# Two-layer convolution block on one core: DRAM buffers cut along their readers, and the inlaid convolution's loads moved from SyncE's queue to ScalarE's

## The chip, the core and the metric

The kernel runs on one core of a Trainium2 chip. The metric is device time in microseconds (us) of one execution; lower is better. Five engines work side by side, each through its own instructions in order: TensorE (PE, with weight loads PEld), VectorE (DVE), ScalarE (ACT), GpSimd (POOL) and SyncE (SP), which here only issues transfers. ACT and POOL issue transfers too. A transfer that must wait for something holds up the engine that issues it, and all that stands behind it there.

## The reference

An input x of 8 x 96 x 96 x 192 passes two blocks, each with a residual. All is float32.

```python
def ema_scan(x, axis):            # s = 0.6 * s + 0.4 * x_t, along one axis
    ...
def block0(x):                    # W_in: 192 -> 384, conv_w: depthwise 3x3, W_out: 384 -> 192
    proj = jnp.einsum('bhwd,dc->bhwc', gn(x), W_in) + b_in
    local = depthwise3x3(proj, conv_w)
    mixed = 0.25 * (lr + rl + tb + bt) + local     # four scans of local: both ways along w and h
    normed = layernorm(mixed, eps=1e-5) * ln_g + ln_b
    return x + jnp.einsum('bhwc,cd->bhwd', normed, W_out) + b_out
def block1(x):                    # 7x7 depthwise on 192 channels, then 192 -> 768 -> 192
    y = depthwise7x7(gn(x), dw_kernel) + dw_bias
    y = layernorm(y, eps=1e-6) * ln_gamma + ln_beta
    y = gelu(jnp.einsum('bhwc,cd->bhwd', y, w0) + b0)
    return x + (jnp.einsum('bhwd,dc->bhwc', y, w1) + b1) * gamma
# gn: 32 groups of 6 channels, over height, width and group, per image, eps=1e-5
```

## The kernel before

The work runs in five stages, with DRAM buffers between them because each stage wants another axis on the partitions.

**First pass (A).** For each image b (8 of them) and each quarter k of the row blocks, x is normalized, turned and multiplied by W_in. `store_a` (L417 and L435) writes the result `po` to the DRAM buffer `P_d`. One `P_d` holds all: two groups g of four images, 384 channels (three parts m of 128), rows and halo rows. POOL issues the writes. For the very last `po` the parts m go out on POOL, POOL and SP, and the halo row on SP.

**3x3 convolution and scans (B).** 96 steps k of four channels. `load_b(k)` asks SP for a weight band (L608) and the input `pin` (L613): per image group g the 32 rows and two halo rows. Convolutions (L626) go to ACT (L635), then to two scans on DVE (L659, L668), each 128 x 768 elements. Three steps are asked for ahead.

**Layer norm and W_out (C).** The result goes to `X1_d`.

**7x7 convolution, first half (D).** The convolution works on 32 blocks n, 16 for each half hf of the images; a block is 12 channels (two groups). A block takes three raw tiles (`load_raw`, t = 0, 1, 2: two transfers each, L839), a weight band (`load_band`, L849), 24 scalings to `xin` (L871 on ACT, L873 on DVE), a copy of the band to the other half of the partitions (`spread`, L877, DVE), six convolution steps (`conv_d`, L1196, evacuated by ACT to `yo`, L1206) and the store of `yo` to `Y_d[hf]` (`store_d`, L1222 to L1227, six transfers on SP). The first N1 = 19 blocks run alone.

**Two-layer network (E), with the other 13 blocks inlaid.** 36 tiles n of y, two rounds u each. `load_y` asks SP for 40 transfers (L1255, L1261) into `ya` and `yb`, each double-buffered. The norm's steps run mostly on DVE (its first is `sums`, L1338) one tile ahead; `turn_in` (L1386, DVE) turns y; `first_layer` (L1401, L1411) makes hp, ACT applies gelu (L1420), `second_layer` (L1431) follows, and DVE adds the residual (L1442). A round has five places where `slot()` is called. While blocks are left, `slot()` takes the next entry of the list `slots`: nine entries per block, three for the scalings and six for the convolution steps. It then takes up to seven steps of the list `loads`, which holds the y transfers that are due.

The order on each engine is the order of these calls (`manual_schedule`); there is no other planner. A tile that reuses memory waits for the last reader of what lay there. In the inlaid stretch SP's one queue therefore carries, in this order of calls, raw tiles, y pieces, bands, residual tiles r (L1276) and stores. The late blocks have two raw buffers, one band, one xin and one yo:

```python
slots[-3].append(lambda n=n: load_raw(n, NT - 1))
if more:
    for t in range(NT - 1):
        slots[t - 2].append(lambda n=n, t=t: load_raw(n + 1, t))
```

Of the kernel before, what the change touches and what calls it, by code (L numbers as in the profile page):

```python
# [8 lines left out]
F32 = mybir.dt.float32  # L9
# [92 lines left out]
def conv_blocks_kernel(  # L102
# [41 lines left out]
    GS = D // GROUPS  # L144

    const = ctx.enter_context(tc.tile_pool(name="const", bufs=1))
    dram = ctx.enter_context(tc.tile_pool(name="dram", bufs=1, space=DRAM))
# [4 lines left out]
    NJ = S // RB  # L152
    P_d = dram.tile([NG, C, RB + 2, GB, NJ, S], F32, name="P_d")
    CS = 2 * C // 3
# [13 lines left out]
    ]  # L168
    Y_d = [dram.tile([ROWS, GROUPS, NH, NV, GS * WQ], F32, name=f"Y_{hf}") for hf in range(2)]

# [33 lines left out]
    ab_pool = ExitStack()  # L204
    mp = ab_pool.enter_context(tc.tile_pool(name="ab_const", bufs=1))
    mix = mp.tile([128, NJ, 128], F32, name="mix")
# [31 lines left out]
    with ExitStack() as ph:  # L238
        cp = ph.enter_context(tc.tile_pool(name="a_const", bufs=1))
        xp = ph.enter_context(tc.tile_pool(name="a_x", bufs=6))  # L240
        sp = ph.enter_context(tc.tile_pool(name="a_small", bufs=2))
        tp = ph.enter_context(tc.tile_pool(name="a_t", bufs=2))
        op = ph.enter_context(tc.tile_pool(name="a_out", bufs=2))
        zp = ph.enter_context(tc.tile_pool(name="zprep", bufs=1))
        ps_t = ph.enter_context(tc.tile_pool(name="a_ps_t", bufs=2, space=PSUM))
        ps_m = ph.enter_context(tc.tile_pool(name="a_ps_m", bufs=2 * NC, space=PSUM))

        avg = cp.tile([S, 128], F32, name="avg")
        nc.vector.memset(avg, 1.0 / S)
        win = cp.tile([128, 3, C], F32, name="win")  # L250
        for p, k, c in spans:
            nc.scalar.dma_start(win[p, k], W_in[c])
        bin_ = cp.tile([128, NC], F32, name="bin_")
        with nc.allow_non_contiguous_dma(reason="one bias per partition"):
# [157 lines left out]
        def store_a(po, b, k):  # L412
            at, g = b % GB, b // GB
            final = b == B - 1 and k == NK - 1

            def whole(m, eng):
                eng.dma_start(  # L417
                    P_d[
                        g, m * 128 : (m + 1) * 128, k * WA : (k + 1) * WA, at
                    ].rearrange("p r j h -> p r (j h)"),  # L420
                    po[:, m].rearrange("p r j h -> p r (j h)"),
                )

            whole(0, nc.gpsimd)
            if not final:
                for m in range(1, NC):
                    whole(m, nc.gpsimd)

            for edge, r, row, js in (
                (NK - 1, WA - 1, RB, (0, NJ - 1)),  # L430
                (0, 0, RB + 1, (1, NJ)),
            ):
                if k == edge:
                    to = slice(1 - js[0], NJ - js[0])
                    (nc.sync if final else nc.gpsimd).dma_start(  # L435
                        P_d[g, :, row, at, to].rearrange("(m p) j h -> p m (j h)", p=128),
                        po[:, :, r, js[0] : js[1]].rearrange("p m j h -> p m (j h)"),
                    )
            if final:
                for m in range(1, NC):  # L440
                    whole(m, (nc.sync, nc.gpsimd)[m % 2])

        def zero_edge(i):

            g, m, e = i // (2 * NC), i // 2 % NC, i % 2
            nc.gpsimd.dma_start(
                P_d[g, m * 128 : (m + 1) * 128, RB + e, :, e * (NJ - 1)], zero
            )
# [49 lines left out]
        with tc.manual_schedule():  # L498
# [13 lines left out]
            for b in range(B):  # L512
                more = b + 1 < B
                for t in range(n_t):
# [40 lines left out]
                    if j == NJ - 1:  # L555
                        store_a(po, b, k)
                if more:
# [12 lines left out]
    NI = len(place)  # L570
    by_tile = dict(reuse_waits="tile")
    gn_pool = ExitStack()
# [15 lines left out]
    with ExitStack() as ph:  # L588
# [12 lines left out]

        def load_b(k):
            c = slice(k * CC, (k + 1) * CC)
            band = bp_.tile([128, CC, 3, RB], F32, tag="band", name=f"band0_{k}")
            pin = bp_.tile([128, CC, GB, NJ, S], F32, tag="pin", name=f"pin_{k}")
            for g in range(NG):
                p = g * 64
                nc.sync.dma_start(  # L608
                    band[p : p + RB + 4].rearrange("p c t o -> p (c t o)"),
                    ZB_d[:, c].rearrange("r c t o -> r (c t o)"),  # L610
                )
                for lo, hi in ((0, RB), (RB, RB + 1), (RB + 1, RB + 2)):
                    nc.sync.dma_start(  # L613
                        pin[p + lo : p + hi].rearrange("p c b j h -> p c (b j h)"),
                        P_d[g, c, lo:hi].rearrange("c r b j h -> r c (b j h)"),
                    )
            return band, pin

# [73 lines left out]
        with tc.manual_schedule():  # L692
            loads = [load_b(k) for k in range(3)]
            locs, lasts, zs, mos, todo = {}, {}, {}, {}, []
# [119 lines left out]
    N1 = NI + 3  # L814
    d_pools = [early, None]
    raws, bands, xins, yos = {}, {}, {}, {}

    def load_raw(n, t):

        hf, i = todo[n]  # L820
        if n >= N1 or ((n == 0 or n % 2) and t < NT - 1):
            pool, bufs = early, NT - 1
        elif n == 0 or n % 2:
            pool, bufs = gp, 1
        else:
            pool, bufs = d_pools[1], NT
        raw = pool.tile([128, NH, NV, GC, WQ], F32, tag="raw", name="raw", bufs=bufs)
        raws[n, t] = raw
        row = NGC * NV * GC * WQ
        run = NV * GC * WQ  # L830
        x1 = X1_d[hf]
        engs = (nc.sync, nc.gpsimd) if n < 2 else (nc.gpsimd,) * 2 if n < N1 else (nc.sync,) * 2
        for g, eng in enumerate(engs):
            src = bass.AP(
                tensor=x1.tensor,
                offset=x1.offset + (2 * t + g) * HG * PH * row + i * run,
                ap=[[row, 64], [ROWS * row, NH], [1, run]],
            )
            eng.dma_start(  # L839
                raw[g * 64 : (g + 1) * 64].rearrange("q b a c v -> q b (a c v)"), src  # L840
            )

    def load_band(n):

# [3 lines left out]
        g = i % 2  # L848
        nc.sync.dma_start(  # L849
            band[g * 64 : (g + 1) * 64].rearrange("q c l -> q (c l)"),  # L850
# [363 lines left out]
    def store_d(n):  # L1214
# [5 lines left out]
        for k in range(2):  # L1220
            y_d = Y_d[hf][:, 2 * i + k].rearrange("r b a n -> r (b a n)")
            nc.sync.dma_start(  # L1222
# [11 lines left out]
    def load_y(n):  # L1234

        hf, p, a, j = place(n)
        y = Y_d[hf][(NJ3 - 1 - j) * PH + PH - 1 - p :: NJ3 * PH]
        main = CK // GS
# [7 lines left out]
        def piece(q, b, eng):  # L1246
# [7 lines left out]
            if b < NH:  # L1254
                eng.dma_start(  # L1255
                    dst[:, b, :cut].rearrange("i (g n) -> i g n", g=main),
                    y[:, chunk * main : (chunk + 1) * main, b, a],
                )
            else:
                g, c = divmod(chunk * (CK - main * GS), GS)  # L1260
                eng.dma_start(  # L1261
                    dst[:, :, cut:],
                    y[:, GROUPS - 2 + g, :, a, c * WQ : (c + CK - main * GS) * WQ],
                )
# [190 lines left out]
    with tc.manual_schedule():  # L1455
# [56 lines left out]
        gn_pool.close()  # L1512
        yp = ctx.enter_context(tc.tile_pool(name="e_yT", bufs=2, side="right", **by_tile))
        rp = ctx.enter_context(tc.tile_pool(name="e_r", bufs=2, side="right", **by_tile))
        tp = ctx.enter_context(tc.tile_pool(name="e_t", bufs=2, side="right", **by_tile))

        slots = []
        for n in range(N1, len(todo)):
            more = n + 1 < len(todo)
            scales = scale_steps(n)  # L1520
            per_t = len(scales) // NT
            slots += [scales[:per_t], scales[per_t : 2 * per_t], scales[2 * per_t :]]
            slots[-3].append(lambda n=n: load_raw(n, NT - 1))
            if more:
                for t in range(NT - 1):
                    slots[t - 2].append(lambda n=n, t=t: load_raw(n + 1, t))
            slots += [[lambda n=n, c=c: conv_d(n, c, ps_y)] for c in range(GS)]
            slots[-1].append(lambda n=n: store_d(n))
            if more:
                slots[-1].append(lambda n=n: load_band(n + 1))  # L1530

        loads = []

        def slot():

            if slots and u >= 2:
                for step in slots.pop(0):
                    step()
            for step in loads[:7]:
                step()  # L1540
            del loads[:7]

# [7 lines left out]
        for u in range(n_u + 1):  # L1550
# [27 lines left out]
            second_layer(u - 1, 2, pool)  # L1578
            turn_in(u + 1, 1)
            if t == 0 and n + 2 < n_y and u < n_u:  # L1580
                assert n + 2 < n_y // 2 or not slots
                assert not loads
                loads += load_y(n + 2)
            chain.pop(0)()
            slot()
            if early_half:
# [52 lines left out]
```

## Time and profile before

| | us |
|---|---|
| median of 3 runs (lowest to highest) | 5541.16 (5528.82 to 5553.41) |
| profiled execution: time | 5532.09 |
| profiled execution: span of its trace | 5530.3 |
| PE busy in the span | 5295.1 (96%) |
| DVE, ACT, POOL busy | 3600.3, 2587.0, 2317.4 |

The trace covers one execution. A busy PE row means that matmuls were under way, not that PE ran at full clock: a table by stretches of time also gives the clock that PE was granted (PEclk, 1.00 is full) and the share of the time in which the transfer engines were busy. "A <- B" in a list of waits means that A stood idle until B ended. A row "SPq" is SP issuing a transfer. Places in the span are given in us from its start: A ends near 753, B near 1790, C near 2628, the first 19 blocks of D near 2945, the inlaid blocks near 4030.

### The profile page before, as it was taken

What the parts mean: (1) busy time and instruction counts of PE and PEld (TensorE: products, weight loads), DVE (VectorE), ACT (ScalarE), POOL (GpSimd) and SP (SyncE); (2) the same over time, 40 slices, a digit from 0 to 9 for tenths busy, and PEclk for the clock granted to TensorE, in tenths of its full rate; (3) what the DMA queues carried; (4) which work ended last, traced back from release to release, by engine and by line L of the source; (5) the groups of instructions that cost most, each with busy time, mean ns of one, the idle gap of its engine ahead of it and who ended that gap; (6) DMA issues with size and microseconds to landing.
All of it is one profiled execution on the core that took longest, in us unless ns stands there. A gap on an engine that the chain in (4) does not pass through costs nothing. (4 is left out here: it accounts for less than half of the span.)

```text
span 5530.3 us, 108052 instructions
## 1 busy us (share of the span) xinstructions
PE 5295.1 (96%) x42206; PEld 3366.3 (61%) x42206; DVE 3600.3 (65%) x6722; ACT 2587.0 (47%) x5778; POOL 2317.4 (42%) x2021
## 2 busy tenths in 40 slices
PE   6999989999999999999788999999999999999999
PEld 4666643333333899899445555666566667767767
DVE  6656449999999455555556555555467777667764
ACT  2444447777777566565435444444433332332332
POOL 1111128888888455555322222222233333333332
PEclk9999989999999999999899999999999999999999
DMA  7999879999997899899996555555433233333331
GB/s 224 286 289 268 237 195 244 246 241 247 243 245 209 256 291 290 266 286 300 294 281 164 119 121 127 125 134 131 111 91 82 80 80 78 83 94 83 80 79 40
DMA packets 793774, 1015.27 MB, mean 184 GB/s; under 512 B 330623, under 2 KB 669696, under 8 KB 791216
## 3 DMA queue, kind: packets, MB, share of 16 engines
q1 hardware_dynamic: 700104, 673.23, 47.8%
q0 software_dynamic: 82976, 331.44, 18.4%
q8 instruction: 333, 5.46, 0.4%
q10 hardware_dynamic: 10184, 3.70, 0.3%
q14 instruction: 177, 1.45, 0.1%
HBM read 603.70 MB, written 419.95 MB: 185 GB/s over the span
## 5 line engine op out<-in xcount | busy, mean ns | idle before, releaser
L1431 PEld LDWEIGHTS hp<-w1g,g 128*128 128x128 f32 x6912 | 1118.6, 190 | 141.4 <-issue 74.0
L1431 PE MATMUL hp<-w1g,g 128*128 128x192 f32 x6912 | 1175.6, 329 | 0.0
L1420 ACT ACTIVATE g<-hp,b0g 128x512 f32<-128x512 f32 x864 | 518.3, 690 | 1149.9 <-PE hp L1411 1149.8
L1450 POOL DMA_DIRECT2D out_dram<-xo x288 | 210.5, 731 | 1647.9 <-DVE xo L1442 1554.0
L1401 PE MATMUL hp<-yT,w0w 128*128 128x512 f32 x1728 | 781.1, 598 | 10.8 <-DVE yT L1386 10.8
L1442 DVE TENSOR_TENSOR xo<-hp,r 128x384 f32<-128x384 f32 x288 | 227.5, 790 | 816.4 <-PE hp L1431 812.1
L1032 PE MATMUL po<-wc,mt 128*128 128x193 f32 x3456 | 688.0, 335 | 9.1 <-DVE x1c L1049 9.1
L626 PE MATMUL pl<-pin,band 34*32 34x380 f32 (+1 forms) x13824 | 628.7, 490 | 20.4 <-DMA pin<-P_d 20.4
L700 POOL TENSOR_TENSOR mo<-mo,z 128x768 f32<-128x768 f32 x286 | 597.2, 2088 | 4.4 <-ACT mo L651 0.4
L1032 PEld LDWEIGHTS po<-wc,mt 128*128 128x128 f32 x3456 | 557.3, 192 | 40.5 <-ACT mean L1034 30.2
L1196 PE MATMUL hp<-xin,band 63*64 63x372 f32 (+1 forms) x4608 | 433.4, 510 | 126.7 <-ACT yo L1206 39.6
L1401 PEld LDWEIGHTS hp<-yT,w0w 128*128 128x128 f32 x1728 | 322.5, 191 | 373.5 <-issue 337.8
L659 DVE TENSOR_TENSOR_SCAN z<-decay,loc 128x768 f32<-128x768 f32 x288 | 505.8, 1756 | 46.0 <-ACT loc L635 16.5
L668 DVE TENSOR_TENSOR_SCAN z<-decay,z 128x768 f32<-128x768 f32 x288 | 498.3, 1731 | 0.1
L626 PEld LDWEIGHTS pl<-pin,band 34*32 34x32 f32 x13824 | 232.5, 107 | 398.5 <-issue 395.8
L1365 POOL TENSOR_TENSOR rs<-tot,neg_half 32x32 f32<-32x32 f32 x72 | 394.6, 5481 | 105.0 <-DVE tot L1363 104.8
L647 PE MATMUL pa<-loc,mix 128*32 128x384 f32 x3456 | 431.9, 493 | 0.0
L650 PE MATMUL pa<-last,down 96*32 96x384 f32 x1152 | 426.8, 493 | 0.9 <-ACT mo L651 0.9
L1411 PE MATMUL hp<-yT,w0w 64*128 64x512 f32 x1728 | 419.6, 611 | 0.0
L1196 PEld LDWEIGHTS hp<-xin,band 63*64 63x64 f32 x4608 | 225.1, 141 | 304.5 <-issue 168.4
L1206 ACT ACTIVATE yo<-hp,dwb 128x384 f32<-128x384 f32 x384 | 196.2, 582 | 441.1 <-PE hp L1196 289.0
L635 ACT COPY loc<-pl 128x384 f32<-128x384 f32 x576 | 248.2, 483 | 313.0 <-PE pl L626 313.0
(155 smaller groups left out, 7519.1 us busy)
## 6 DMA issues: line engine op xcount, KB each, us to landing
pin<-P_d SPq DMA_DIRECT2D x192, 576.0 KB
P_d<-po POOLq DMA_DIRECT2D x95, 1152.0 KB, 9.7
mt<-M SPq DMA_DIRECT2D x192, 384.0 KB
xq<-in_x_dram SPq DMA_DIRECT2D x96, 576.0 KB
xr<-in_x_dram SPq DMA_DIRECT2D x192, 288.0 KB
X<-x1c SPq DMA_DIRECT2D x144, 384.0 KB
out_dram<-xo POOLq DMA_DIRECT2D x288, 192.0 KB, 2.6
r<-X SPq DMA_DIRECT2D x35, 1536.0 KB
```

Source lines behind the costliest of these rows:

```text
L626: nc.tensor.matmul(pls[g][at * RB : (at + 1) * RB, :, lo:hi], band[rows, c, kh, :], pin[rows, c, :, NJ - 1 - j, lo + kh - 1 : hi + kh - 1] ...
L647: nc.tensor.matmul(pa[at], mix[:, i, at], loc[:, q], start=True, stop=True)
L650: nc.tensor.matmul(pa[at], down[:, to], last[:, q], start=True, stop=True)
L659: nc.vector.tensor_tensor_scan(zf, decay_f, loc.rearrange("p q n -> p (q n)"), 0.0, ALU.mult, ALU.add)
L668: nc.vector.tensor_tensor_scan(zr, decay_f, zr, 0.0, ALU.mult, ALU.add)
L700: eng.tensor_tensor(m, m, z, ALU.add)
L1032: nc.tensor.matmul(po, lhs[m], wc[:, m], start=(m == 0), stop=(m == NC - 1))
L1196: nc.tensor.matmul(pys[g][k * 64 : (k + 1) * 64, :, lo:hi], band[rows, k * GS + c, d * ZS : d * ZS + 64], xin[rows, :, :, k * GS + c, lo + ...
L1401: nc.tensor.matmul(hps[m, q], w0w[:, 0, m * 128 : (m + 1) * 128], yT[:, 2 * q], start=True, stop=False,)
L1411: nc.tensor.matmul(hps[m, q], w0w[p, 1, m * 128 : (m + 1) * 128], yT[p, 1], start=False, stop=True,)
L1420: nc.scalar.activation(g[:, m, q], hps[m, q], AF.Gelu, bias=b0g[:, m : m + 1], scale=1.0)
L1431: nc.tensor.matmul(po[:, q], g[:, m, q, k * 128 : (k + 1) * 128], w1g[:, m], start=(m == 0), stop=(m == NE - 1),)
```

## The change

1. `P_d` becomes six buffers, one for each group g and part m. The last `po`'s part m = 0 goes out in two halves of 64 partitions, on POOL and on ACT, its halo row on ACT; parts 1 and 2 and their halo rows go out on POOL. Halo rows are stored for each part apart.
2. The memory pools of stage A get `reuse_waits="tile"`, `pin` gets two tags, and stage B's start asks first for group 0 of k = 0 and 1, then for group 1 of k = 0, and so on; within a step the inputs now stand ahead of the band.
3. `Y_d[hf]` becomes seven buffers: six of five groups of channels, as one y piece reads them, and one of two.
4. In the inlaid stretch the raw tiles and bands are asked for by ACT. There are three raw buffers instead of two (the third lies in the pool of yT), and all three tiles of block n + 1 are asked for during block n's scalings. Block 19's third tile is asked for by POOL at the end of D, as its first two now are.
5. `store_d(n)` moves from the end of block n's last slot to the start of the next block's first slot.
6. `slot()` takes up to 14 steps of `loads`, and `load_y` is added after the fourth slot of a round instead of before it.

```diff
-    P_d = dram.tile([NG, C, RB + 2, GB, NJ, S], F32, name="P_d")
+    P_d = [
+        [dram.tile([128, RB + 2, GB, NJ, S], F32, name=f"P_{g}_{m}") for m in range(NC)]
+        for g in range(NG)
+    ]
...
+    YG = 5
+    Y_d = [
+        [
+            dram.tile(
+                [ROWS, min(YG, GROUPS - g), NH, NV, GS * WQ], F32, name=f"Y_{hf}_{g}"
+            )
+            for g in range(0, GROUPS, YG)
+        ]
...
-        xp = ph.enter_context(tc.tile_pool(name="a_x", bufs=6))
+        xp = ph.enter_context(tc.tile_pool(name="a_x", bufs=6, **by_tile))
...
             if final:
-                for m in range(1, NC):
-                    whole(m, (nc.sync, nc.gpsimd)[m % 2])
+                whole(0, nc.gpsimd, slice(0, 64))
+                edges(0, nc.scalar)
+                whole(0, nc.scalar, slice(64, 128))
+                steps = [lambda m=m: whole(m, nc.gpsimd) for m in range(1, NC)]
+                return steps + [lambda m=m: edges(m, nc.gpsimd) for m in range(1, NC)]
...
-            loads = [load_b(k) for k in range(3)]
+            tile_b(2)
+            bands_b[0] = tile_band_b(0)
+            for k in range(2):
+                load_pin_b(k, 0)
+            for k in range(3):
+                for g in range(1 if k < 2 else 0, NG):
+                    load_pin_b(k, g)
+                load_band_b(k)
+            loads = [tiles_b[k] for k in range(3)]
+            for step in late_a:
+                step()
...
-        engs = (nc.sync, nc.gpsimd) if n < 2 else (nc.gpsimd,) * 2 if n < N1 else (nc.sync,) * 2
+        engs = (nc.sync, nc.gpsimd) if n < 2 else (eng or nc.gpsimd,) * 2
...
+        d_pools[2] = yp
+        load_raw(N1, NT - 1)
...
-            slots += [scales[:per_t], scales[per_t : 2 * per_t], scales[2 * per_t :]]
-            slots[-3].append(lambda n=n: load_raw(n, NT - 1))
+            slots += [after + scales[:per_t], scales[per_t : 2 * per_t], scales[2 * per_t :]]
             if more:
-                for t in range(NT - 1):
-                    slots[t - 2].append(lambda n=n, t=t: load_raw(n + 1, t))
+                for t in range(NT):
+                    slots[t - 3].append(lambda n=n, t=t: load_raw(n + 1, t, nc.scalar))
             slots += [[lambda n=n, c=c: conv_d(n, c, ps_y)] for c in range(GS)]
-            slots[-1].append(lambda n=n: store_d(n))
             if more:
-                slots[-1].append(lambda n=n: load_band(n + 1))
+                slots[-1].append(lambda n=n: load_band(n + 1, nc.scalar))
+            after = [lambda n=n: store_d(n)]
+        slots.append(after)
...
-            for step in loads[:7]:
+            for step in loads[:14]:
                 step()
-            del loads[:7]
+            del loads[:14]
...
+            chain.pop(0)()
+            slot()
             if t == 0 and n + 2 < n_y and u < n_u:
                 assert n + 2 < n_y // 2 or not slots
                 assert not loads
                 loads += load_y(n + 2)
-            chain.pop(0)()
-            slot()
```

## The prediction

> **What bounds the kernel now.** I read the stretch table first, one row per stage, to see where PE is not busy; then the lists of waits in those places; then the timeline of one gap. The columns after the length are busy us of PE, PEld, DVE, ACT, POOL, then the clock granted to PE, the transfer engines' share, GB/s.
>
> ```profile
> 753.00:771.00 18.00, 0.64 (x2) 0.18 (x2) 1.41 (x11) 0.57 (x2) 1.33 (x2) 0.57 0.96 268
> 771.00:1788.00 1017.00, 1014.50 (x18368) 351.16 (x18366) 974.13 (x573) 712.01 (x1716) 867.53 (x939) 0.99 0.92 238
> ...
> 2627.60:2945.00 317.40, 244.08 (x2630) 149.90 (x2628) 171.99 (x482) 126.19 (x255) 79.33 (x106) 0.90 0.96 278
> ...
> 2945.00:4030.00 1085.00, 1020.79 (x5622) 630.39 (x5623) 593.11 (x1136) 489.78 (x849) 296.63 (x153) 0.97 0.54 126
> ...
> 4370.00:5530.00 1160.00, 1154.62 (x5260) 809.85 (x5256) 773.25 (x1449) 355.92 (x499) 387.79 (x216) 1.00 0.30 78
> ```
>
> The last stretch is PE at full clock: nothing there can be won by moving transfers. Stage B (second row) is DVE's: 288 pairs of scans at 1.756 and 1.731 us are 1004 of its 1017 us, so B ends a fixed time after its first scan starts. D's first half is held by transfers (0.96). Two places are left: the 18 us between A and B, and the inlaid stretch, where PE idles 64 us and runs at a mean clock of 0.97 with the transfer engines half idle. Its waits, total us, times, longest:
>
> ```profile
> DVE s L1338 <- DMA yb<-Y: 106.6, 13, 17.7
> ...
> ACT xin L871 <- DMA raw<-X: 69.1, 13, 11.5
> ...
> PE hp L1196 <- DVE band L877: 30.3, 4, 10.9
> ...
> PE hp L1196 <- ACT xin L871: 18.8, 6, 6.4
> ```
>
> So PE waits for a block's first convolution (L1196), and behind that stand late y pieces (`sums`, L1338, blocks the band copy queued behind it on DVE) or late raw tiles. One such gap in the timeline:
>
> ```profile
> 3200.31 1.87 SPq L1255 DMA_DIRECT2D yb<-Y  x4
> ...
> 3202.28 1.25 SPq L839 DMA_DIRECT2D raw<-X  x2
> ...
> 3209.33 3.61 ACT L871 ACTIVATE xin<-raw,s 128x192 f32<-128x192 f32 x8 [6.67 <-DMA raw<-X]
> ...
> 3212.63 1.01 DVE L1338 TENSOR_REDUCE s<-yb 128x16 f32<-128x512 f32 x1 [12.49 <-DMA yb<-Y]
> 3213.67 1.45 DVE L877 COPY band<-band 64x2496 f32<-64x2496 f32 x1
> ...
> 3215.27 4.04 PE L1196 MATMUL hp<-xin,band 63*64 63x384 f32 x24 [10.16 <-DVE band L877]
> ```
>
> The reader is to see that raw tile and y pieces are interleaved in SP's one queue, both asked for late, and that the convolution after the gap takes 4.04 us; at full clock 24 such matmuls end and the next group begins after 2.06 (3567.57 to 3569.62).
>
> **What the inlaid stretch would take without gaps.** From 2991 to 4064 (1073 us) lie 26 rounds u and 13 x 6 = 78 convolution steps. A round without convolutions repeats every 32.24 us (L1431 pairs at 4087.14 and 4119.38). 26 x 32.24 + 78 x 2.06 = 999 us: 74 us are lost to gaps and to the half clock after them. A second way: PE issues 1758 matmuls in 317 us from 3495 to 3812, where it never waits over 2 us (5.55 per us), but 2546 in 504 us before (5.05) and 1289 in 252 us after (5.12); at 5.55 the outer two would take 459 and 232, that is 65 us less. Both agree on the size of what is to be had.
>
> **The change, part by part.**
>
> *A to B.* In the trace, the last `po` (ACT and DVE end at 753.6) is written, SP's loads wait and interleave with the writes, and B's first convolutions run at 774.3:
>
> ```profile
> 766.20 0.17 DVE L972 MEMSET blk<- 128x128 f32 x1 [13.18 <-DMA P_d<-po]
> ...
> 769.42 1.57 SPq L613 DMA_DIRECT2D pin<-P_d  x3
> ...
> 774.32 15.50 PE L626 MATMUL pl<-pin,band 34*32 34x384 f32 x190 [2.50 <-DMA pin<-P_d]
> ...
> 779.34 1.76 DVE L659 TENSOR_TENSOR_SCAN z<-decay,loc 128x768 f32<-128x768 f32 x1 [11.59 <-ACT loc L635]
> ```
>
> Group 0's inputs for k = 0, 1 can now land before 753 (the transfer share from 680 to 752 is 0.38 to 0.50). The critical loads, group 1 of k = 0, follow m = 0's write, which now goes on two queues and no longer has m = 2's beside it on SP's ring: written by about 758, loaded by about 764, against pieces landing until 774. But DVE has a memset ahead of the first scan, and in the changed order it (c_pre, the row after blk) waits for all last writes, m = 1 and 2 and their halo rows too, all on POOL now. By 758 about 1.5 of 3.5 MB is written; the rest shares some 330 GB/s (324 to 342 from 756 to 764) with the loads: 2.0 / 0.165 = 12 us, to about 770.5. First scan at about 770.8, against 779.34: -8.5 us, with -12 (scan follows the loads) and -5 (writes squeezed out longer) as ends. POOL issues 32 more halo stores of 0.744 us in A (24 us, beside 111 busy of 753): free, as POOL spends 533 us waiting for ACT's `po`. Were POOL full, `po`'s two buffers would hold up ACT.
>
> *Y_d.* SP's waits around the first y loads (2895 to 2992) name no store of Y for a y load: reads are already tied only to stores that they overlap. 0 (-3 to +3 for another layout of the same rows).
>
> *Raw tiles and bands to ACT, third buffer, tiles a block ahead.* 12 blocks x 6 = 72 raw transfers and 12 bands leave SP. The raw tile, now asked for a block (some 70 us) ahead, is not late; y pieces lose the raw requests standing among them. ACT gets 72 x 0.61 + 12 x 1.39 = 61 us of issuing (SP's durations), over 490 busy of 1085; in the timeline it waits 3.6 us for PE ahead of each group of four gelus, so a pair (1.2 us) fits. Against this stands a rule of the Trainium skill, "DMA: Bandwidth & Descriptors", section "Issuing engines are not separate DMA queues": all issuers end on the same 16 engines, and another issuer only saves issue time. By it the move is worth nothing here, since SP is not short of issue time, and the total is -8.5 alone, about 5533. The rows say otherwise: what is saved is not issue time but the place in the queue. SP stood in front of y loads (L1255) waiting for DVE 728 us in all, with raw requests behind, while ACT waited 69 us. I take the rows and keep the rule for the range.
>
> *What is late next.* Two things stay. In 3495 to 3812, with no late transfer, PE still gave up 3 us in 4.4 blocks, as eight scalings (3.6 us) follow four gelus (2.4 us): about 1 us a block, 13 us. And the eight transfer semaphores turn in call order over SP and ACT together: each new transfer waits for the one eight before. ACT can thus stop for a y piece that SP has not landed. A y tile takes 31 us of SP's time in the last stretch and 34 to 44 in 3495 to 3812; its last calls now stand 24 us after the buffer is free, so an ACT request just behind can wait 5 us or so. What queues behind it are gelus, then PE. Nothing in the trace shows it; below, 0 (the request meets a finished one); above, 4 us a block (a lag of 8 less the 3.6 idle). I take 1 us a block, as slots just behind the last y piece are about one in five: 12 us. So the stretch gives -74 + 13 + 12 = -49 (ends -70 and -10).
>
> *store_d a slot later, y pieces 14 at a time, load_y after the slot.* No instruction is added; DVE's and PE's order stay. The single yo has three slots (24 us) from store to next writing, and the six issues take about 5.5 us (0.33 + 0.35 + 2.05, twice): covered, and if not, ACT's yo waits (16 us now in this stretch). In the last stretch y pieces end 12 us before `sums`: covered.
>
> *Third tile of block 19 by POOL at D's end.* 2.3 MB of raw now start near 2954 beside y_1's pieces (2944 to 2977), which DVE awaits (9 us gap of PE at 2978); at 300 GB/s that is 8 us of traffic. +3 (0 to +8).
>
> **Sum.** -8.5 - 49 + 3 = -54.5, against the profiled execution's 5532.09: 5477.6. The median of the runs, 5541.16, stands 9 above that execution; on it, 5486.7. I forecast 5486 for the median.
>
> **The rivals.**
>
> 1. *All of it goes:* no request on ACT is held, as in the quietest stretch or better. -8.5 - 70 = 5463. For: transfer share 0.54. Against: ACT's bursts ahead of first convolutions remain.
> 2. *The queue was not the cause:* y pieces stay late by their own chain (yb pieces wait for each other, some 4 us per five), and only A to B and a part of raw remain: -8.5 to -20, about 5527. For: yb is the name in the longest waits. Against: from 3583 to 3697 the same chain was in time.
> 3. *ACT becomes the bound* (slower): each block's seven requests wait on SP's y pieces, gelus stand, PE drops to half clock. Its place is a block's three scaling slots; at 9 us a block (6 of gap, 3 of half clock, like the gap above less ACT's idle) 13 blocks cost 117, and 5541 - 54.5 + 117 = 5604. It decides from 54.5 / 13 = 4.2 us a block. For: ACT's queue is in order and semaphores are shared. Against: SP, freed of raws, runs ahead of the calls most of the time.
> 4. *The split does nothing:* if DVE's memset ends with the old writes' time (766) plus loads as now, A to B gives 0: 5495. Inside the first case's range.
>
> **How the numbers follow.** Likeliest case 0.63 (own range 5465 to 5508), rival 1 0.19, rival 2 0.13, rival 3 0.05. Range 5450 to 5522: below, rival 1 with A to B at -12 and a fast run; above, the weak half of rival 2 is left out. This kernel's measurement tells about 0.5% (28 us) from no change: faster by more means under 5513. Faster: 0.63 + 0.19 + 0.07 of rival 2 = 0.89; within: 0.06 of rival 2 and 0.01 of rival 3 = 0.07; slower 0.04.
>
> **What would show it.** First scan of B near 771 and its wait a memset's for the writes of P; SP's rows with no raw from 3000 on; "DVE s <- DMA yb" and "ACT xin <- DMA raw" under 20 us each; gaps of PE ahead of L1196 of 1 to 2 us, clock 0.99 in the stretch; the inlaid blocks ending near 3975 instead of 4030. Wrong: ACT rows at raw requests that wait for y transfers by more than 4 us a block, or y pieces still late with SP free.

## The result, and the profile after

The changed kernel takes 5499.89 us (median of 11 runs, 5494.79 to 5531.08), the kernel before, run beside it, 5537.92 us (11 runs, 5527.56 to 5553.70). The ratio is 0.9935, with a 95% interval of 0.9918 to 0.9953. The profiled execution took 5497.31 us (span 5495.5); that of before, 5532.09. So some 35 to 38 us went, where 54.5 were forecast.

The stretches of the changed kernel, with the same bounds and columns as those shown of before (busy us of PE, PEld, DVE, ACT, POOL; granted clock; transfer share; GB/s):

```profile
753.00:771.00 18.00, 1.81 (x12) 0.78 (x8) 2.80 (x11) 2.10 (x4) 3.57 (x5) 0.66 0.83 252
771.00:1788.00 1017.00, 1015.71 (x18368) 354.97 (x18368) 974.32 (x574) 711.82 (x1716) 868.01 (x939) 0.99 0.91 237
2627.60:2945.00 317.40, 244.43 (x2643) 148.18 (x2643) 175.86 (x491) 130.28 (x264) 80.68 (x107) 0.88 0.96 279
2945.00:4030.00 1085.00, 1042.71 (x5775) 649.16 (x5774) 580.41 (x1176) 499.39 (x858) 321.02 (x165) 0.98 0.52 127
```

Only the last row has moved much: PE issues 5775 matmuls there where it issued 5622. The list of waits for 2945 to 4030 (total us, times, longest) has no row any more of ACT's scaling waiting for a raw tile (69.1 us before):

```profile
DVE s L1388 <- DMA yb<-Y: 58.0, 9, 19.6
...
PE hp L1244 <- DVE band L925: 18.8, 1, 18.8
...
PE hp L1244 <- ACT xin L919: 3.9, 5, 1.6
```

One gap of 18.8 us still stands in it, and another of 18.4 us lies ahead of it (PE waiting for DVE's `yT`): both at E's start. From 3076 to 4030 the first of these rows is only this:

```profile
DVE s L1388 <- DMA yb<-Y: 20.5, 6, 10.2
```

To compare kernels stage by stage I use times at which DVE ends the last transpose (L1386 before, L1436 after) of a y tile. At that time its buffer is free for the y tile two later, so "y_3's buffer free" in the expectations is when y_1 has been turned (also called "y_1's free" there). All in us, read to about 0.1:

| kernel | A's last matmul to B's first scan | E's first matmul to y_0 turned | to y_1 turned | to y_13 turned | rest |
|---|---|---|---|---|---|
| before | 26.9 | 30.6 | 67.1 | 1006.3 | 1465.6 |
| after | 23.4 | 39.1 | 76.8 | 954.2 | 1466.3 |
| difference | -3.5 | +8.5 | +9.7 | -52.1 | +0.7 |

What is left of the -34.8 of the spans is +2.3 in A (PE starts at 41.5 instead of 39.85), +0.9 in B, +1.8 in C and -3.2 in D. So a gain of 52 us in the inlaid stretch was there, and 18 were given back at E's start.

**The step from A to B, after.** The timeline:

```profile
754.89 2.50 POOL L430 DMA_DIRECT2D P<-po  x3 [18.23 <-ACT po L421]
...
760.47 4.26 SPq L644 DMA_DIRECT2D pin<-P  x3
764.83 3.26 SPq L631 DMA_DIRECT2D band<-ZB_d  x2
...
772.29 8.44 PE L662 MATMUL pl<-pin,band 34*32 34x384 f32 x90 [17.48 <-issue]
774.91 0.17 DVE L1027 MEMSET c_pre<- 128x128 f32 x1 [17.09 <-DMA P<-po]
777.30 0.86 ACT L671 COPY loc<-pl 128x384 f32<-128x384 f32 x2 [21.41 <-PE pl L662]
778.19 1.76 DVE L695 TENSOR_TENSOR_SCAN z<-decay,loc 128x768 f32<-128x768 f32 x1 [3.12 <-ACT loc L671]
```

The reader is to see that the memset waits for the last writes as foretold, but is done 3 us before the scan: the scan waits for ACT's copy, and that for the convolution. What the convolution waits for this list does not name; the loads in front of it are issued from 760 on, and e2_band_first below names them.

**E's start, after.** Two events, in one timeline:

```profile
2951.16 3.73 POOL L887 DMA_DIRECT2D raw<-X  x6
...
2953.41 2.20 SPq L1305 DMA_DIRECT2D yb<-Y  x4
2972.58 0.30 SPq L1311 DMA_DIRECT2D yb<-Y  x1
...
2986.26 1.01 DVE L1388 TENSOR_REDUCE s<-yb 128x16 f32<-128x512 f32 x1 [17.73 <-DMA yb<-Y]
2994.22 2.05 PE L1451 MATMUL hp<-yT,w0w 128*128 128x512 f32 x2 [18.44 <-DVE yT L1436]
...
3030.85 15.91 SPq L1305 DMA_DIRECT2D yb<-Y  x4
...
3041.41 1.28 ACTq L887 DMA_DIRECT2D raw<-X  x2
...
3048.43 0.30 SPq L1311 DMA_DIRECT2D yb<-Y  x1
...
3059.20 1.00 DVE L1388 TENSOR_REDUCE s<-yb 128x16 f32<-128x512 f32 x1 [19.61 <-DMA yb<-Y]
3070.87 1.46 DVE L925 COPY band<-band 64x2496 f32<-64x2496 f32 x1
3072.47 3.96 PE L1244 MATMUL hp<-xin,band 63*64 63x384 f32 x24 [18.79 <-DVE band L925]
```

First event: POOL asks for block 19's raw tiles at 2951, and the next piece of y_1's yb can be asked for only 19.2 us after the first four (2953.41 to 2972.58); before, with those raws on SP behind the y pieces, 8.7 us (2957.06 to 2965.80). Whether the raws are the cause is tested below. Second event: the row at 3030.85, an ask for four pieces of y_2, takes SP 15.9 us, nearly all of it one wait ahead of the fourth. What it waits for is in SP's own list of waits (2991 to 3076):

```profile
SPq L1305 <- DMA raw<-X: 14.2, 1, 14.2
```

That piece reads and writes nothing of raw. What ties it to raw is the semaphore that tells of a transfer's landing. In the trace the transfers of SP and of ACT use the same eight in turn (numbers 100 and 102 to 108), those of POOL eight others (111 to 118). The piece has to wait for number 108, and the transfer that had it last, eight before in order of calls, is ACT's raw request. ACT issues that only at 3041.41, between two bursts of scaling.

### The profile page after: what moved, and what is told of

It is laid out like the page before. It is cut to its first block, busy times and chain, and to the rows that moved or that the text cites. A ratio compares the mean times of both kernels' runs of the same rounds, so it can differ in the third digit from the quotient of the medians.

```text
span 5495.5 us, 108054 instructions
## 1 busy us (share of the span) xinstructions
PE 5277.4 (96%) x42206; PEld 3357.6 (61%) x42206; DVE 3449.8 (63%) x6722; ACT 2586.1 (47%) x5778; POOL 2367.0 (43%) x2060
## 5 line engine op out<-in xcount | busy, mean ns | idle before, releaser
L1244 PE MATMUL hp<-xin,band 63*64 63x372 f32 (+1 forms) x4608 | 420.7, 501 | 95.7 <-ACT yo L1254 35.2
L395 PE MATMUL pm<-xT,win 128*128 128x384 f32 x1152 | 392.4, 491 | 0.0
```

Of the source, the lines that this page charges most:

```text
L1244: nc.tensor.matmul(pys[g][k * 64 : (k + 1) * 64, :, lo:hi], band[rows, k * GS + c, d * ZS : d * ZS + 64], xin[rows, :, :, k * GS + c, lo + ...
```

## Experiments

Every run is compared with the kernel before on the same chip in the same session; "run on SP" is e1_raw_sp.

**e1_p_only.** The parts for `P_d`, `store_a` and B's first loads alone, on the kernel before:

```
+        [dram.tile([128, RB + 2, GB, NJ, S], F32, name=f"P_{g}_{m}") for m in range(NC)]
...
+                whole(0, nc.gpsimd, slice(0, 64))
+                edges(0, nc.scalar)
+                whole(0, nc.scalar, slice(64, 128))
...
+            for k in range(2):
+                load_pin_b(k, 0)
...
```

> Only the first pass's buffers and the order of stage B's first loads are taken from the change; Y's buffers and the inlaid convolution stay as before. Theory (the gain is all in the inlaid stretch, and the step from A to B gave 1 to 4 us because the band of k = 0 now stands behind two waiting pin loads): first scan of B 1 to 4 us earlier counted from A's last matmul, whole time -4 to +4 us, ratio 0.9993 to 1.0007. If the later start of C seen after the change (+3.6 us) comes from this part, C's first matmul stands 3 to 5 us later here too and the ratio is near 1.0005; if it comes from elsewhere, C moves with the scan. Rival (the forecast's term, -8.5 us, was right and the other 5 us were lost elsewhere): ratio 0.9985.

Measured: 5535.19 us, ratio 0.9998 (0.9985 to 1.0011); A's last matmul to the first scan 23.5 us; the inlaid stretch 1008.4. This part is worth 3.4 us of 5540, below what whole times resolve. C starts 12.6 us later in its profiled execution, because B took 1030.8 us instead of 1017.5; the last section shows such lengths of B without these edits too.

**e1_e_only.** The inlaid edits alone, without the split of P and Y:

```
+            pool, bufs = d_pools[2], 1
+                    slots[t - 3].append(lambda n=n, t=t: load_raw(n + 1, t, nc.scalar))
+                slots[-1].append(lambda n=n: load_band(n + 1, nc.scalar))
+            after = [lambda n=n: store_d(n)]
+            for step in loads[:14]:
...
```

> Only the inlaid convolution's edits are taken (requests on ScalarE, third raw tile, a block ahead, y pieces 14 at a time, store a slot later); the DRAM buffers and stage B's loads stay as before. Theory: the whole gain is here: -52 us in the steady stretch, +16 to +20 us at E's start, so -30 to -38 us, ratio 0.993 to 0.9945. Rival (the split of Y is what frees the y pieces): -10 to -20 us, ratio 0.9965 to 0.998.

Measured: 5504.98 us, ratio 0.9942 (0.9925 to 0.9960), with 40.6, 76.7 and 954.4 us in the three stages of E: those of the changed kernel. The split of Y does nothing that shows.

**e1_raw_sp and e1_raw_pool.** The changed kernel with the inlaid raws and bands asked for by SP, and by POOL:

```
-                    slots[t - 3].append(lambda n=n, t=t: load_raw(n + 1, t, nc.scalar))
+                    slots[t - 3].append(lambda n=n, t=t: load_raw(n + 1, t, nc.sync))      # or nc.gpsimd
-                slots[-1].append(lambda n=n: load_band(n + 1, nc.scalar))
+                slots[-1].append(lambda n=n: load_band(n + 1, nc.sync))                    # or nc.gpsimd
```

> The changed kernel, but the inlaid blocks' raw tiles and bands are asked for by SP again; third raw tile, the block's lead and the y pieces' 14 at a time stay. Theory 1 (the place in SP's queue is the cause, as forecast): raws again stand among y pieces and wait for buffers there; 'DVE s <- DMA yb' comes back to 60 to 100 us, and 30 to 45 us of the gain are given back: ratio to before 0.999 to 1.002. Theory 2 (the lead of a block and the third tile are the cause, the queue is not): the steady stretch stays within 10 us of the changed kernel's, and y_2's late piece at E's start, which waited for ScalarE's raw request, comes sooner: ratio 0.990 to 0.9945.

> The changed kernel, but the inlaid blocks' raw tiles and bands are asked for by GpSimd, whose transfers count on semaphores of their own. Theory (SP's and ScalarE's shared eight semaphores hold y_2's piece behind ScalarE's raw request at E's start): the second long gap of PE at E's start (18.8 us, at about 3054) shrinks to 10 us or less, with the half clock after it: 8 to 18 us faster than the changed kernel, ratio to before 0.990 to 0.992. Rival (y_2's pieces are late from traffic and order alone, or GpSimd's requests come late behind its own waits): gap stays above 15 us, ratio 0.993 to 0.996.

Measured: SP 5479.28 us, ratio 0.9896 (0.9879 to 0.9912); POOL 5482.28 us, ratio 0.9893 (0.9877 to 0.9909). To y_1 turned: 60.0 and 59.8 us instead of 76.8; to y_13 turned: 952.2 and 951.2 instead of 954.2. Putting everything back into SP's queue loses nothing and wins 17 us at E's start. With the other edits in place, the queue in which the raw requests stand is not what gains: there the forecast's cause is refuted (e3_queue_only asks the same of the kernel before). The second gap at E's start, 18.8 us of PE, was the price of ScalarE's requests.

**e2_blk20_sp.** One request is enough to show the place of that price:

```
-   load_raw(n + 1, t, nc.scalar)
+   load_raw(n + 1, t, nc.sync if n == N1 else nc.scalar)
```

> The changed kernel, with only the first inlaid block's requests for the next block's raw tiles moved from ScalarE to SP; all later ones stay on ScalarE. Theory (the loss on ScalarE is one event: y_2's piece waits for the ScalarE request eight transfers ahead, issued late): from y_0's buffer free to y_1's free 60 to 63 us instead of 76.8, later stretch unchanged at 952 to 956, so 14 to 17 us faster than the changed kernel: ratio to before 0.990 to 0.991. Rival (the coupling meets the next block instead): the same loss appears one or two y tiles later, ratio 0.993 to 0.994.

Measured: 5479.57 us, ratio 0.9906 (0.9889 to 0.9924); 60.3 us to y_1 turned and 953.7 to y_13. Where PE waited 18.79 us it now waits 2.38:

```profile
3064.26 3.61 PE L1244 MATMUL hp<-xin,band 63*64 63x384 f32 x24 [2.38 <-DVE band L925]
```

The loss was one event, at the first block; the raw requests of the other eleven blocks and all bands, still on ScalarE, cost nothing that shows. The coupling itself goes on: from 3076 to 4064 SP's y pieces (L1305) wait for raw transfers 49.8 us in 17 waits in the changed kernel, against 15.7 us in 11 in the run on SP, for a stretch only 2 us longer.

**e3_queue_only.** The kernel before, with the move to ScalarE alone:

```
-        engs = (nc.sync, nc.gpsimd) if n < 2 else (nc.gpsimd,) * 2 if n < N1 else (nc.sync,) * 2
+        engs = (nc.sync, nc.gpsimd) if n < 2 else (nc.gpsimd,) * 2 if n < N1 else ((nc.sync, nc.scalar)[n > N1],) * 2
...
-        nc.sync.dma_start(
+        (nc.sync, nc.scalar)[n > N1].dma_start(
```

> The kernel before, with one edit: from block 20 on, raw tiles and bands are asked for by ScalarE. Third raw tile, lead and y pieces as before. Theory (the forecast's cause, SP's queue, is not it; the third tile's short lead and the y pieces' pace are): from y_3's buffer free to y_15's free 995 to 1015 us (before 1006), ratio 0.999 to 1.004. Rival (the queue is a cause too, and lead and pace are two more ways to the same gain): 960 to 985 us, ratio 0.992 to 0.997.

Measured: 5534.28 us (22 runs), ratio 1.000 (0.999 to 1.001), 1002.5 us to y_13 turned. So the move to ScalarE gives nothing in the whole and at most 4 us in its stretch. This is a balance: in the trace SP's y pieces (L1255) wait 45.7 us for raw transfers from 3076 to 4064, against 6.5 before. The same move to POOL, whose transfers share no semaphore with SP's, was not run on the kernel before; on the changed kernel POOL and SP differ by 1 us (951.2 and 952.2).

**e2_lead_only and e3_pieces_only.** The run on SP with one half of the other inlaid edits each. Lead only keeps the third raw buffer and its tile's lead of a block; besides the lines shown, `load_y` is called ahead of the slot again:

```
-            for step in loads[:14]:
+            for step in loads[:7]:
-            after = [lambda n=n: store_d(n)]
+            slots[-1].append(lambda n=n: store_d(n))
```

> As the run with raws asked for by SP, and with the y pieces 7 at a time, their start and the store's slot also put back as before: of the edits in the inlaid stretch only the third raw buffer and the third tile's lead of a block are left. Theory (that lead alone is the cause): from y_3's buffer free to y_15's free stays within 952 to 962 us (before 1006, changed 954), whole time within 8 us of the run on SP. Rival (the y pieces' rate and place hold half of it): 970 to 990 us in that stretch, 15 to 30 us slower than the run on SP.

Pieces only keeps what this undoes, and undoes what it keeps (block 19's raw tiles are asked for by SP again, too):

```
-            pool, bufs = d_pools[2], 1
-                for t in range(NT): slots[t - 3].append(lambda n=n, t=t: load_raw(n + 1, t, nc.sync))
+            slots[-3].append(lambda n=n: load_raw(n, NT - 1))
+                for t in range(NT - 1): slots[t - 2].append(lambda n=n, t=t: load_raw(n + 1, t))
```

> As the run with raws asked for by SP, but without the third raw buffer and the third tile's lead of a block: of the inlaid edits only the y pieces 14 at a time, their start a slot later and the store a slot later are left, with all requests on SP. Theory (the two parts add: lead 22, pieces 32 of 54 us): 968 to 982 us from y_3's to y_15's buffer free, ratio 0.993 to 0.996. Rival (both are needed for the gain of either beyond 22): 990 us or more, ratio over 0.997.

Measured: lead only 5511.96 us, ratio 0.9957 (0.9941 to 0.9973), 983.9 us to y_13 turned; pieces only 5511.15 us, ratio 0.9956 (0.9943 to 0.9969), 982.5 us. Against 1006.3 before, each is worth 22 to 24 us, and both together 54 (952.2): they add, with 8 us more that only both give. In the first of the two the rival I had set against "lead alone" came true (33 us slower than the run on SP, a little more than its 15 to 30); the second ended at the edge of its theory (982.5 against 968 to 982).

The waits from 3076 to 4064 tell the two apart. Before:

```profile
DVE s L1338 <- DMA yb<-Y: 91.4, 12, 17.7
ACT xin L871 <- DMA raw<-X: 62.4, 12, 11.5
...
PE hp L1196 <- DVE band L877: 21.5, 3, 10.9
```

Move to ScalarE alone:

```profile
DVE s L1338 <- DMA yb<-Y: 103.2, 12, 17.7
PE hp L1196 <- DVE band L877: 38.8, 5, 15.4
```

Lead only:

```profile
DVE s L1388 <- DMA yb<-Y: 91.1, 11, 17.2
PE hp L1244 <- DVE band L925: 23.5, 5, 9.1
```

Pieces only:

```profile
ACT xin L917 <- DMA raw<-X: 37.4, 4, 13.4
PE hp L1242 <- ACT xin L917: 24.6, 6, 8.3
DVE s L1386 <- DMA yb<-Y: 18.6, 4, 10.3
```

The reader is to see two separate troubles. Late raw tiles go with the lead; late y pieces go with the pace; the move alone took away the raw wait, and PE then waited longer for the band copy that stands behind the y pieces. Why the pieces were late is in SP's own waits of the same stretch, before, move alone, lead only and pieces only:

```profile
SPq L1222 <- ACT yo L1206: 217.4, 13, 22.0
...
SPq L1255 <- DVE yT L1386: 96.6, 7, 22.5
```

```profile
SPq L1222 <- ACT yo L1206: 212.1, 13, 19.8
```

```profile
SPq L1271 <- ACT yo L1254: 205.0, 13, 19.2
```

```profile
SPq L895 <- PE hp L1242: 199.2, 12, 40.8
...
SPq L1269 <- ACT yo L1252: 4.9, 9, 0.6
```

In the first three SP stands some 16 us a block in front of the store of Y (`store_d`), which waits for ACT's `yo`, with y pieces behind it. Before, in one block (y_4's pieces, SP alone):

```profile
3166.01 0.91 SPq L1255 DMA_DIRECT2D yb<-Y  x2
3183.24 0.32 SPq L1222 DMA_DIRECT2D Y<-yo  x1
...
3193.88 1.44 SPq L1255 DMA_DIRECT2D yb<-Y  x2
```

From first to last issue y_4's 40 pieces take 70.3 us before, and 77.2 and 69.5 in the next two. With 14 a slot and the store a slot later they are out before SP meets that store (32.0 us in the run on SP), and in pieces only SP does its waiting at the next band. Not every tile gets through so fast (y_6's pieces still take 63.0 us in the run on SP), but DVE's wait for yb falls to 18.6 us in pieces only and 28.1 on SP.

The wait for `yo` need not go for that. In the changed kernel, where the bands are on ACT, SP still stands at the store:

```profile
SPq L1271 <- ACT yo L1254: 151.3, 11, 21.6
```

Yet y_4's pieces take 31.8 us there, and the stretch is as short as on SP (954.2 and 952.2). What counts is what stands behind the wait. Which does more, the 14 a slot, `load_y` after the slot or the later store, was not run apart.

**e2_band_first.** The run on SP, band 0 ahead of group 1's pins:

```
+            first = load_band_b(0)
             for k in range(3):
                 for g in range(1 if k < 2 else 0, NG): load_pin_b(k, g)
-                load_band_b(k)
+                if k: load_band_b(k)
```

> As the run with raws asked for by SP, but at B's start band 0 is asked for ahead of group 1's pin loads, not behind them. Theory (band 0 stood behind two loads that wait for the last writes, so B's first convolution came late): from A's last matmul to the first scan 19 to 21.5 us instead of 23.8. Rival (the pin load or DVE's memset behind the last writes ends the gap anyway): 23 to 24 us, and the memset or the pin is the row's wait.

Measured: 5481.62 us, ratio 0.9913 (0.9896 to 0.9929); 24.2 us from A's last matmul to the scan, as without it. Its timeline:

```profile
763.62 6.55 SPq L646 DMA_DIRECT2D pin<-P  x6
...
773.31 12.33 PE L664 MATMUL pl<-pin,band 34*32 34x384 f32 x152 [18.39 <-DMA pin<-P]
773.64 0.17 DVE L1032 MEMSET c_pre<- 128x128 f32 x1 [16.47 <-DMA P<-po]
...
778.33 1.76 DVE L697 TENSOR_TENSOR_SCAN z<-decay,loc 128x768 f32<-128x768 f32 x1 [4.53 <-ACT loc L673]
```

The band was not the last: the pin is, issued at 763.6 after the write of m = 0 and used 9.7 us later. So that write and that load bound this step. That the load is slow because of the other writes beside it is likely, but no run tests it.

**e2_late19 and e3_blk19_sp.** The run on SP, with block 19's third tile asked for by POOL a round later; and with all three by SP, behind y_1's pieces:

```
-        load_raw(N1, NT - 1)
+            if u == 1: load_raw(N1, NT - 1)          # late19
-                load_raw(N1, t)
+                load_raw(N1, t, nc.sync)             # blk19_sp, and so for the third
```

> As the run with raws asked for by SP, but block 19's third raw tile is asked for a round later (u = 1) instead of at D's end. Theory (its 0.77 MB beside y_1's pieces cost the first rounds of E): from E's first matmul to y_0's buffer free goes from 39.6 back to 30 to 33 us, with the half clock after it 6 to 10 us in all, ratio to before 0.988. Rival (the pieces of y_1 are late by their own chain, and the first gap only moves into a wait for the raw tile at u = 2): same time within 3 us, or slower.

> As the run with raws asked for by SP, and block 19's three raw tiles are asked for by SP too, in the same place of the program: they stand behind y_1's pieces and the last stores, as two of them did before, instead of starting beside y_1's pieces from GpSimd's queue. Theory (2.3 MB beside y_1's yb pieces made the first gap of E): from E's first matmul to y_0's buffer free 29 to 32 us instead of 39.6, gap of PE 8 to 10 us; 6 to 10 us faster than the run on SP, ratio 0.988 to 0.9895. Rival (the three tiles now come between y_1 and y_2 and make y_2's pieces or block 19's scaling late): from y_0's to y_1's buffer free goes from 60 to 67 to 72, same time as the run on SP.

Measured: late19 5483.47 us, ratio 0.9912 (0.9896 to 0.9929), with 36.8 + 61.7 = 98.5 us to y_1 turned, against 99.6 on SP; blk19_sp 5486.42 us, ratio 0.9924 (0.9901 to 0.9947), with 29.7 + 70.2 = 99.9. Two misses that teach the same: the traffic was the cause of the first gap (29.7 instead of 39.6), and it only moved into y_2's pieces (70.2 instead of 60.0).

**e4_after_bias.** So the three tiles were put between the two:

```
-                load_raw(N1, t)
-        load_raw(N1, NT - 1)
         bias_r(0)
+        for t in range(NT):
+            load_raw(N1, t)
```

> As the run with raws asked for by SP, and GpSimd asks for block 19's three raw tiles only after it has added the bias to r_0, some 30 us later than at D's end: behind y_1's pieces and ahead of y_2's. Theory (2.3 MB of raw beside y_1's yb pieces open the first gap of E; the same 2.3 MB between y_1 and y_2, as in the run with block 19 on SP, only move it into y_2's pieces; in between there is room): from E's first matmul to y_0's buffer free 29 to 32 us and from there to y_1's free 60 to 63 us, sum 89 to 95 instead of 99.6; 5 to 10 us faster than the run on SP, ratio 0.987 to 0.989. Rival (the stores of y and r_0 fill that room too): the sum stays at 98 to 102 us, ratio as of the run on SP.

Measured: 5480.63 us (5465.60 to 5497.33), ratio 0.9890 (0.9871 to 0.9909); 29.5 + 61.0 = 90.5 us to y_1 turned and 952.2 to y_13. PE's first gap is 8.8 us again, with the raws asked for after y_1's last piece (3001.40):

```profile
3004.79 3.73 POOL L887 DMA_DIRECT2D raw<-X  x6
...
3011.98 2.05 PE L1451 MATMUL hp<-yT,w0w 128*128 128x512 f32 x2 [8.76 <-DVE yT L1436]
```

The stages are 9 us better than on SP; the whole time does not show it (0.9890 against 0.9896, intervals overlapping). Executions differ by more than that in B, as told below: in the two traces B took 1042.1 us here and 1017.4 on SP. Both intervals lie below that of the changed kernel.

## Why the prediction was right, and where it was not

The direction and the range held: 5499.89 us, within 5450 to 5522, where 5486 was forecast. The place held too: A to B and the inlaid stretch, and nothing in the last one. The mechanism held in part only. That the total came so near is partly luck: what the gaps were worth had been counted rightly, but about half of it was won by edits that I had put at 0, and the move to ScalarE, which I gave the credit, cost 16 us (115.9 us from E's first matmul to y_1 turned, 99.6 with the requests on SP).

- **The inlaid stretch, -49.** From y_0 turned to y_13 turned it took 1031.0 us instead of 1073.4: -42.4, made of -52.1 and +9.7. The gain's size came out, and one of its causes, the third tile's lead of a block, is right: 22 us alone, 30 beside the other edits. But the step on which the choice of queue rested failed: "what is saved is not issue time but the place in the queue", read as the place of the raw requests. e3_queue_only shows that move alone worth nothing (1.000), and the run on SP that undoing it loses nothing. The rows that I took for it were misread. The 728 us of L1255's wait for DVE are those of the whole execution (28 waits); from 3076 to 4064 they are 96.6 us, and 627 us come after 4064, where no raw request is left: that is only SP being early. I set them against 69 us of ACT in the inlaid stretch alone. The row that held y pieces up there was "SPq L1222 <- ACT yo", 217 us.
- **"store_d a slot later, y pieces 14 at a time": 0.** This was the mis-sized term. "No instruction is added" was true; that the pieces pass the waiting store was not seen. It measures 24 us alone, 32 beside the lead (983.9 to 952.2).
- **The rule on issuing engines.** The Trainium skill, "DMA: Bandwidth & Descriptors", section "Issuing engines are not separate DMA queues", says that another issuer saves only issue time. For the move it was right, with 1.000 measured, and I was wrong to set it aside; the total of 5533 that I drew from it was wrong, because it took the other edits as worth nothing.
- **ACT's requests, 1 us a block.** Over the later blocks 2 us in all against SP (954.2 to 952.2), not 12. The coupling by the shared semaphores was real, but what it cost went the other way: SP's y piece waited for ACT's late request, once with effect, 14.2 us that made y_1 17 us later. I had looked at what the moved request waits for, and not at who now waits for it. Rival 3 priced the right mechanism in the wrong direction.
- **Block 19's tiles, +3 (0 to +8).** At E's first gap +8.5 (39.1 against 30.6 us; 9.6 against e4_after_bias), near the 8 us of traffic that I counted. But the term forgot that the tiles cost as much where they had stood: with SP asking for them behind y_1's pieces the sum to y_1 turned is 99.9 us, with POOL at D's end 99.6. So this move by itself came to about 0, and the 18 us given back at E's start are nearly all ACT's requests (16).
- **A to B, -8.5.** Measured -3.5 counted from A's last matmul, and -1.15 at the first scan. The write of m = 0 let SP's load of it go at 760 to 764, not 758 (760.5 in the changed kernel, 763.6 in e2_band_first), and the load, in the latter, was used 9.7 us after its issue, not 6. The memset was late (774.9, where the forecast had it done by 770.5), but not last, so rival 4's place was right and its mechanism not.
- **Y_d, 0.** As predicted: e1_e_only is at 0.9942 without it.
- **Rival 2.** Its chain of yb pieces is still there (from 3076 to 4064 SP's L1311 waits 149.7 us for yb after, L1261 147.4 before), and does no harm when it starts in time. It had the queue right and the remainder wrong.

Of the signs named beforehand, SP without raws, no raw wait of ACT and the clock came (1.00 from 3076, 0.98 over the stretch with E's start); "DVE s <- DMA yb" was 58.0 us, not under 20, because of E's start; the first scan was at 778.2, not 771; the inlaid convolutions end at 3981.6 (4017.1 before).

## What to carry to other kernels

When transfers in an in-order queue are late, ask of every waiting row ahead of them whether something urgent stands behind it; a store that waits for its producer holds up loads as surely as a late load, and letting the loads past it was worth as much here as a third buffer. Moving requests to another engine by itself gave nothing, and made SP wait for ScalarE's requests through shared completion semaphores: look at who waits for the moved request, too. Check that a total of waits belongs to the stretch that you argue about. Large prefetches belong into a stretch where no urgent transfer is under way; here 2.3 MB cost some 10 us in one place, 9 in the next, and nothing between them (stages of one trace each).

## What was not expected of the hardware

After the gap between A and B, PE's clock stays at half for a time that differs between executions of the same instructions, though PE is busy from 772 on. In eight of the fourteen traces the half clock lasts 34 to 38 us, in the other six 55 to 79. Rows for 771 to 900 of the changed kernel, of e1_p_only and of e4_after_bias (the number behind POOL's is the clock):

```profile
771.00:900.00 129.00, 127.71 (x2184) 47.69 (x2188) 113.95 (x68) 82.58 (x200) 89.33 (x98) 0.92 0.88 218
```

```profile
771.00:900.00 129.00, 127.29 (x1968) 45.40 (x1976) 102.10 (x61) 75.00 (x180) 79.50 (x87) 0.82 0.79 195
```

```profile
771.00:900.00 129.00, 127.73 (x1799) 43.56 (x1803) 93.26 (x56) 68.05 (x163) 70.49 (x77) 0.74 0.74 178
```

Full clock comes back at 792.7, 817.7 and 837.4 us. Until then, in the slower two and after three faster ones, a pair of scans takes 6.7 us instead of 3.5, since the convolution feeds them too slowly (its matmuls take 840 ns instead of 484), and from B's first scan to its last takes 1018.4, 1030.8 and 1042.1 us. It is seen in kernels with the old loads as well (e3_queue_only, 814.3 us and 1026.7). So executions differ by 12 to 24 us in B though the kernels of the three rows run the same instructions there, and the prediction's "B ends a fixed time after its first scan starts" holds only where the clock comes back at the same time. Edits worth under 10 us are therefore read from their own stage. What sets the length is open.
